# Loads and writes of ternary weight pieces on ScalarE, all seven quarters of the context kept, and another order in the last batch

## The chip, the cores and the metric

The kernel runs on one core of a Trainium2 chip. The metric is the device time of one execution in microseconds (us). The kernel before took 3075.5 us (median of three runs, 3074.82 to 3080.68). The profiled execution took 3074.66 us; its span in the trace is 3072.2 us, so that 2.46 us lie around the span.

The engines are called PE (TensorE, matmuls), PEld (its weight loads), DVE (VectorE), ACT (ScalarE), POOL (GpSimd) and SP (SyncE, which mostly issues DMAs). Each works through its own instructions in a fixed order; a waiting instruction holds up all that stands behind it on its engine.

## The reference

The reference is a model of two layers on `x` (8 batches, 64 rows, 512 columns) and a context `ctx` (8, 1601, 512), with a residual sum around each part:

```python
    x = x + _L0_xattn_ref(_layernorm(x, axis=-1), ctx_1024, mask, Wq, Wkv, Wout, b_out)
    x = x + _L0_attn_ref(_layernorm(x, axis=-1), ...)     # low frequencies attend, high ones are convolved
    x = x + _L0_ffn_ref(_layernorm(x, axis=-1), ...)      # eight experts, a few tokens each
    x = x + _L1_xattn_ref(_layernorm(x, axis=-1), ctx_1024, ctx_1024, ...)
    x = x + _L1_attn_ref(_layernorm(x, axis=-1), ...)     # relative positions
    x = x + _L1_ffn_ref(_layernorm(x, axis=-1), w1, b1, w2, b2)
```

The argument lists are shortened here. Three parts matter for the change. The first cross-attention (16 heads of 64) and the second (16 heads of 32, with a layer norm over each head's queries and keys) both read all of the context. The last part quantizes its two weights (2048 x 512 and 512 x 2048) to three values:

```python
def weight_quant(w):
    scale = 1.0 / jnp.clip(jnp.mean(jnp.abs(w)), 1e-05)
    q = jnp.clip(jnp.round(w * scale), -1.0, 1.0) / scale
    return w + jax.lax.stop_gradient(q - w)
```

So the mean of the absolute values of a whole weight is needed (measure) before any of its elements can be rounded (round).

## The kernel before

The kernel is one program of six stages: `l0_xattn` (0 to about 1505 us in the profile), `l0_attn` (to 1590), the experts (to 1850), `l1_xattn` (to 2907) and a tail with the second layer's attention and feed-forward part (to 3072). A list scheduler decides the order of each engine's instructions from priorities and dependencies; the program text gives the order in which operations become known to it. `tc.keep_in_program_order(ins)` holds one instruction behind the one written just before it on the same engine; the instructions that use its result are not held.

**Quarters.** The large products with the context are done with seven multiplications for two by two blocks in place of eight. For a pair of 128-row blocks of the context the tile `q` holds seven quarters of 128 x 256: four are loaded, and `Quarters.left` (L134 to L139) makes the three others and overwrites one, with four additions on GpSimd. `Quarters.LEFT` (L131) says which of the seven stands where. The matmuls of L468 (scores) and L585 (values) use the quarters, ACT copies some products out of PSUM (`p`, `u` of L428, L531), and DVE adds them up (`s` of L433, `a` of L553 to L568).

**First cross-attention.** The loop at L648 has 17 steps. Step `2*b + half` makes the scores of one half of the heads of batch `b` (`scores`, L420 to L480, six pairs of blocks, run.add once a pair), then its softmax (`softmax` from L496), while the values of the step before are attended (`attend`, L570 to L625, four parts with pieces). `load_columns(b, keep)` (L177) loads the six pairs of the transposed context for a step, 12 DMAs of 256 KB, and has GpSimd make the other quarters, in both halves. In the first half (`keep`) it also writes four of the quarters of each pair to memory (`kept`, two DMAs of 128 and 384 KB a pair). `load_rows` (L194) loads the pairs of the context's rows for the values. Both take their tiles from the same pool of six. The queries, multiplied by the key weight, come through memory as `qk` (L227, 1024 KB), and GpSimd makes their four sums `qt` (L219 to L222).

**The maximum.** `top_of` transposes the running maximum `m` (L449) on PE (`m_ps`, L486), reduces it (`top`, L488) and spreads it with a matmul (`top_ps`, L491); the subtraction (L501) and Exp (L502) follow, and sums that prepare the values (L508 to L511, L515).

**Ternary weights.** The two weights of the last part come in 16 pieces of 512 KB (`TernaryWeights`, L1859). `pass_by` loads a piece from SP into one of two buffers. `measure` (L1887) sums absolute values on ACT (Abs, L1889). `round` (L1900) scales and rounds a piece on DVE (L1904, float32), turns it into bf16 on ACT into the tile `wq` (L1905), limits it to -1 and 1 on DVE (L1906, bf16) and writes it back from SP. There is one buffer of `wq`. `aside(step)` (L363) calls `measure` twice a step in steps 2 to 9 and `round` three times a step in steps 10 to 15; it stands at the end of a step (L668). In the trace these come in bursts: Abs at 240 to 246, 388 to 396 and 415 to 449 us, the rounding at 1015 to 1057, 1074 to 1088 and 1100 to 1147 us.

**Second cross-attention.** `load(b, g)` (L1430) fetches two pairs of blocks (one of three groups of a batch) with eight DMAs: the raw quarters from the input, the made ones from `kept`. The loop over the batches ends (L1802 to L1836) with the work on four score tiles `s[0]` to `s[3]` (four heads each): `scores` (L1684, matmuls of L1691, DVE L1701), `softmax` (a maximum by `fold`, L1709 to L1714, its transpose L1722, `top` L1724, the subtraction L1733, Exp L1734, and a second fold for the total) and `attend` (L1742, with the sum of L1751 and its reciprocal L1754). Three tiles `s` exist. In the last batch (`more` is false) nothing of a next batch stands between these.

Of the kernel before, what the change touches and what calls it, by code (L numbers as in the profile page):

```python
# [123 lines left out]
class Quarters:  # L124
# [5 lines left out]

    LEFT = {1: 0, 2: 1, 3: 6, 4: 3, 5: 4, 6: 5, 7: 2}  # L131

    @staticmethod
    def left(nc, q):  # L134

        nc.gpsimd.tensor_add(q[:, 4, :], q[:, 2, :], q[:, 3, :])  # L136
        nc.gpsimd.tensor_sub(q[:, 5, :], q[:, 4, :], q[:, 0, :])
        nc.gpsimd.tensor_sub(q[:, 2, :], q[:, 0, :], q[:, 2, :])
        nc.gpsimd.tensor_sub(q[:, 6, :], q[:, 1, :], q[:, 5, :])  # L139


def l0_xattn(K, x, d, ternary, kept):
# [7 lines left out]
    with ExitStack() as es:  # L150
# [25 lines left out]

        def load_columns(b, keep=False):  # L177

            pairs = []
            for i in range(NPAIR):  # L180
                q = cp.tile([P, 7, QH], F32, tag="pair", name="ctxT")
                for j in range(2):
                    nc.sync.dma_start(
                        q[:, ds(2 * j, 2), :].rearrange("p h (c n) -> p (h c) n", n=P),
                        d["ctxT"][b, :, ts(2 * i + j, P)].rearrange("(c p) n -> p c n", p=P),
                    )
                Quarters.left(nc, q)
                if keep:
                    nc.sync.dma_start(kept[b][:, i, 3, :], q[:, 2, :])
                    nc.sync.dma_start(kept[b][:, i, 0:3, :], q[:, 4:7, :])  # L190
                pairs.append(q)
            return pairs

        def load_rows(b):  # L194

            pairs = []
            for i in range(NPAIR):
                q = cp.tile([P, 7, QH], F32, tag="pair", name="ctx")
                for j in range(2):
                    nc.sync.dma_start(  # L200
                        q[:, 0:4, :].rearrange("p (h j) n -> p j h n", j=2)[:, j],
                        d["ctx"][b, ts(2 * i + j, P), :].rearrange("p (h n) -> p h n", n=QH),
                    )
                Quarters.left(nc, q)
                pairs.append(q)
            return pairs
# [103 lines left out]
        load_tails(0)  # L310
        ctxT = load_columns(0, True)
        place = [tp.tile([P, 4, 3, QH], F32, tag="pt", name="stage").rearrange("p a b q -> p (a b q)") for _ in range(2)]
# [49 lines left out]

        def aside(step):  # L363
            if 2 <= step < 10:
                for i in range(2):
                    ternary.measure(piece, 2 * (step - 2) + i)
            if step == 10:
                ternary.scales(ps_m.tile([P, 16], F32, tag="mm", name="w_ps"), ones[:, 0:1])
            if 10 <= step < 16:
                for i in range(3 * (step - 10), min(3 * (step - 9), 16)):  # L370
                    ternary.round(piece, zp, i)

# [78 lines left out]
        def scores(b, qkt, ctxT):  # L451
# [12 lines left out]
            for i in range(NPAIR):  # L464

                def mul(ps, n, start, i=i):
                    for e in range(2):
                        nc.tensor.matmul(  # L468
                            ps,
                            lhsT=ctxT[i][:, Quarters.LEFT[n], ts(e, P)],  # L470
                            rhs=right[n][:, e, :],
                            start=start and e == 0,
                            stop=e == 1,
                            skip_group_check=not start,
                        )

                run.add(mul, Scores(s, m, b, i))
                some(2)
            run.end()
            return s, m  # L480
# [89 lines left out]
        def attend(half, s, soft, ctx, o, first):  # L570
# [8 lines left out]
            for part, right in enumerate(parts):  # L579
                pairs = range(3 * part, 3 * part + 3)  # L580
                for m in range(2):
# [22 lines left out]
                    run.add(mul, Mixed(a, m, part == 0, tail))  # L604
                    some(2 * part)
            run.end()
            a5 = a.rearrange("p c (g h q) -> p c g h q", h=2, q=S)
# [40 lines left out]
        for step in range(2 * B + 1):  # L648
            if step < 2 * B:
                b, half = divmod(step, 2)  # L650
                if step:
                    now, ctxT = queries_of(b, half), load_columns(b, half == 0)
                    if half == 0:
                        nc.sync.dma_start(
                            ctxT_tail[:, :, :TAIL], d["ctxT"][b, :, LAST * P :].rearrange("(c p) n -> p c n", p=P)
                        )
                s, m = scores(b, now, ctxT)
                top = top_of(m)
                if step == 1:
                    between = keys_side_of_rest(columns_of(norm_rest, NT - 1))  # L660
# [5 lines left out]
            if step < 2 * B:  # L666
                before = s, softmax(s, top)
            aside(step)  # L668
            if step == 3:
                some(5 * NG)  # L670
            if step and step % 4 == 0:
                project_out(step // 4 - 1, o)
                if step < 2 * B:
                    o = tp.tile([P, NG, 2, S], F32, tag="o", name="o", bufs=1)


# [725 lines left out]
def l1_xattn(K, x, d, ahead, queries_done, in_last, kept):  # L1402
# [7 lines left out]
    with ExitStack() as es:  # L1410
# [19 lines left out]
        def load(b, g):  # L1430

            q = cp.tile([P, 2, 7, QH], F32, tag="ctxT", name="ctxT")
            for u in range(2):
                i = 2 * g + u
                nc.sync.dma_start(
                    q[:, u, 0:2, :].rearrange("p h (c n) -> p (h c) n", n=P),
                    d["ctxT"][b, :, ts(2 * i, P)].rearrange("(c p) n -> p c n", p=P),
                )
                nc.sync.dma_start(
                    q[:, u, 3, :].rearrange("p (c n) -> p c n", n=P),  # L1440
                    d["ctxT"][b, SET:, ts(2 * i + 1, P)].rearrange("(c p) n -> p c n", p=P),
                )
                nc.sync.dma_start(q[:, u, 2, :], kept[b][:, i, 3, :])
                nc.sync.dma_start(q[:, u, 4:7, :], kept[b][:, i, 0:3, :])
            return q
# [237 lines left out]

        def scores(c, r):  # L1684

            s = sp.tile([P, NK, 4, S], F32, tag="s", name="s")
            for k0 in range(0, NK, 2):
# [27 lines left out]

        def softmax(s):

# [13 lines left out]
            for k0, n in (0, 7), (7, NK - 7):  # L1731
                part = s[:, ds(k0, n)]
                nc.vector.tensor_sub(part, part, top.to_broadcast([P, n, 2 * P]))  # L1733
                nc.scalar.activation(part, part, AF.Exp)  # L1734
            total = tp.tile([P, 2 * P], F32, tag="total", name="total")
            fold(s, ALU.add, total)
            return total

        def attend(c, s, total, acc, rs):
# [34 lines left out]
        for b in range(B):  # L1774
# [41 lines left out]
            values(1, 1)  # L1816
            total[2] = softmax(s[2])
            values(2, 0)
            values(2, 1)
            s[1] = scores(1, r_of[1])  # L1820
            keys(0, (0, 1))
            total[1] = softmax(s[1])
            attend(0, s[0], total[0], acc, rs)
            s[3] = scores(3, r_of[3])
            if more:
                queries_of(b + 1, 1)
                queries_of(b + 1, 3)
            keys(0, (2,))
            finish(0)
            attend(2, s[2], total[2], acc, rs)  # L1830
            total[3] = softmax(s[3])
            keys(1, (0,))
            attend(1, s[1], total[1], acc, rs)
            keys(1, (1, 2))
            finish(1)
            attend(3, s[3], total[3], acc, rs)  # L1836
            if b % 2 == 0:
# [21 lines left out]
class TernaryWeights:  # L1859
# [5 lines left out]
    def __init__(self, K, pool, memory, d):  # L1865
        nc = self.nc = K.nc
        self.down = pool.tile([P, 1], F32, tag="wdown", name="wdown")
# [11 lines left out]
    def pass_by(self, piece, i):  # L1879
        w = piece([D], "wraw").rearrange("p a b -> p (a b)")  # L1880
        self.nc.sync.dma_start(self.shaped(w, i), self.from_[i])
        return w
# [3 lines left out]

    def measure(self, piece, i):  # L1887
        w = self.pass_by(piece, i)
        self.nc.scalar.activation(w, w, AF.Abs, accum_out=self.part[:, i // 8, i % 8 : i % 8 + 1])  # L1889
# [9 lines left out]

    def round(self, piece, pool, i):  # L1900
        nc, n = self.nc, i // 8
        w = self.pass_by(piece, i)
        q = pool.tile([P, 1024], BF16, tag="wq", name="wq")
        nc.vector.tensor_scalar(w, w, self.scale[:, n : n + 1], MAGIC, ALU.mult, ALU.add)  # L1904
        nc.scalar.activation(q, w, AF.Identity, bias=self.down, scale=1.0)  # L1905
        nc.vector.tensor_scalar(q, q, 1.0, -1.0, ALU.min, ALU.max)  # L1906
        nc.sync.dma_start(self.to[i], self.shaped(q, i))

# [354 lines left out]
def program(tc, d):  # L2263
    nc = tc.nc
    with tc.tile_pool(name="const", bufs=1) as cp, tc.tile_pool(name="memory", bufs=1, space=DRAM) as memory:
# [4 lines left out]
        slots, done = (memory.tile([CAP * E_, D], F32, tag=n, name=n) for n in ("slots", "done"))  # L2270
        kept = [memory.tile([P, NPAIR, 4, QH], F32, tag=f"kept{b}", name="kept") for b in range(B)]
        l0_xattn(K, x, d, w, kept)
# [128 lines left out]
```

## Time and profile before

| what | us |
|---|---|
| median of three runs (lowest to highest) | 3075.5 (3074.82 to 3080.68) |
| the profiled execution, and its span | 3074.66, span 3072.2 |
| Abs of one piece on ACT (L1889, 16 of them) | 1.057 |
| rounding of one piece: DVE L1904, ACT L1905, DVE L1906 | 0.752, 1.148, 0.426 |
| a DMA issue on ACT | 0.35 to 0.44 |
| one addition of `Quarters.left` on GpSimd (L136, ctxT) | 0.814 |
| from issue to landing, median: ctxT 256 KB, ctx 256 KB, kept written 384 KB | 4.7, 3.2, 2.8 |
| last batch: `m` of the last score tile ready (DVE L1714), last Exp's attend starts | 2888.7, 2895.1 |

The execution was profiled at a mean granted TensorE clock of 0.989 of full speed. The granted clock is half of full speed in these stretches (us): 70.9 to 77.8, 94.8 to 101.7, 1101.8 to 1108.6, 1129.1 to 1132.5, three short ones between 1535 and 1590, 2886.9 to 2900.6, and four more after 2907.

In the profile, "busy" is the time in which an engine executes; issuing a DMA and waiting do not count. A line such as `PE a L1 <- DVE b L2: 4.0, 1, 4.0` says that PE's instruction of line 1 writing `a` found its engine idle and waiting for what DVE did in line 2: 4.0 us in total, once, 4.0 us the longest. In a timeline the first two columns are start and duration, and the bracket is the idle time before with what ended it. 391.76 MB are moved by DMA in an execution.

### The profile page before, as it was taken

To read this page: it belongs to the slowest core of one execution; us is meant where nothing else is said; L and a number is where in the kernel's file an instruction comes from. 1 tells how busy PE (TensorE), PEld (TensorE's weight loads), DVE (VectorE), ACT (ScalarE), POOL (GpSimd) and SP (SyncE) were. 2 spreads that over 40 slices of the span, in tenths; PEclk is the share of its full clock that TensorE was granted. 3 is DMA by queue.
4 is the path that set the end of the run, shared out by engine and by line. 5 is a ranking of instruction groups with operands and counts; after the bars stand their busy time and mean duration, and the time that the engine had idled before them with its cause. 6 is when DMAs were issued, how large, how long until landed. Compare 5 with 4: busy or idle time off the path is not lost.

```text
span 3072.2 us, 41098 instructions
## 1 busy us (share of the span) xinstructions
PE 2979.5 (97%) x15516; PEld 2287.8 (74%) x15521; DVE 1827.7 (59%) x3124; ACT 843.2 (27%) x1618; POOL 993.9 (32%) x959
## 2 busy tenths in 40 slices
PE   8999999999999989999999999999999999999887
PEld 7777768888888768888654446788788888888654
DVE  4845545666656656665443333487676676576648
ACT  2322241222222322222111222233333333323224
POOL 4433343544454534544110002322422404214010
PEclk9999999999999999999999999999999999999899
DMA  8265474434334564432659974212112021030270
GB/s 264 71 198 150 150 245 126 138 104 142 127 103 129 183 192 134 129 116 73 221 186 337 344 265 145 78 30 75 40 54 77 5 89 52 28 89 4 72 122 14
DMA packets 387187, 391.76 MB, mean 128 GB/s; under 512 B 55054, under 2 KB 289558, under 8 KB 385838
## 3 DMA queue, kind: packets, MB, share of 16 engines
q1 hardware_dynamic: 380761, 371.80, 39.4%
q10 hardware_dynamic: 5589, 15.24, 1.4%
q8 instruction: 123, 2.02, 0.3%
q0 software_dynamic: 640, 2.10, 0.2%
q14 instruction: 74, 0.61, 0.1%
HBM read 332.90 MB, written 56.16 MB: 127 GB/s over the span
## 4 chain that ended last, share of the span: by engine, by line
PE 57%; DVE 3%; DMA 2%; ACT 1%; issue 0%; POOL 0%; SPq 0%; POOLq 0%; ACTq 0%; DVEq 0%
PE x_ps L1528 11%; PE y_ps L1528 8%; PE s_ps L1691 6%; PE h_ps L1204 4%; PE oe_ps L1231 4%; PE acc L1742 4%; PE x_ps L585 3%; PE x_ps L468 2%; PE z_ps L585 2%; PE z_ps L468 1%; PE sum_ps L1575 1%; PE y_ps L585 1%; PE y_ps L468 1%; DMA wo<-in_L1x_Wp 1%; PE vt_ps L1619 1%; PE top_ps L1727 1%
## 5 line engine op out<-in xcount | busy, mean ns | idle before, releaser
L1588 POOL TENSOR_TENSOR r<-r,minus_half 128x52 f32<-128x52 f32 x32 | 276.9, 8672 | 559.2 <-DVE r L1587 559.2
L468 PE MATMUL x_ps<-qt,ctxT 128*128 128x256 f32 x1152 | 286.2, 382 | 10.5 <-ACT u L428 7.6
L585 PE MATMUL x_ps<-pt,ctx 128*128 128x256 f32 x1152 | 281.7, 382 | 6.2 <-DVE a L561 4.9
L468 PEld LDWEIGHTS x_ps<-qt,ctxT 128*128 128x128 f32 x1152 | 217.3, 190 | 51.2 <-ACT u L428 10.3
L585 PEld LDWEIGHTS x_ps<-pt,ctx 128*128 128x128 f32 x1152 | 217.2, 190 | 40.2 <-DVE a L561 5.0
L136 POOL TENSOR_TENSOR ctxT<-ctxT 128x256 f32<-128x256 f32 x96 | 78.1, 814 | 415.5 <-DMA ctxT<-in_ctxT 336.0
L1691 PE MATMUL s_ps<-qb,kT 128*128 128x256 f32 x832 | 201.2, 381 | 0.0
L449 DVE TENSOR_TENSOR m<-m,s 128x512 f32<-128x512 f32 x176 | 138.1, 785 | 93.7 <-ACT s L447 91.1
L136 POOL TENSOR_TENSOR ctx<-ctx 128x256 f32<-128x256 f32 x96 | 73.6, 767 | 342.7 <-DMA ctx<-in_ctx 262.6
L1691 PEld LDWEIGHTS s_ps<-qb,kT 128*128 128x128 f32 x832 | 154.2, 190 | 26.2 <-issue 3.5
L501 DVE TENSOR_TENSOR s<-s,top_ps 128x1024 f32<-128x1024 f32 (+1 forms) x112 | 123.2, 1135 | 22.9 <-PE top_ps L491 22.9
L1733 DVE TENSOR_TENSOR s<-s,top_ps 128x1792 f32<-128x1792 f32 x64 | 117.9, 1884 | 28.8 <-PE top_ps L1727 28.8
L433 DVE SCALAR_TENSOR_TENSOR s<-y_ps,bias,p 128x256 f32<-128x256 f32 x96 | 46.3, 483 | 145.9 <-PE y_ps L468 145.1
L1701 DVE TENSOR_TENSOR s<-s_ps,r 128x512 f32<-128x512 f32 x192 | 126.5, 682 | 10.8 <-PE s_ps L1691 10.2
L1734 ACT ACTIVATE s<-s 128x1792 f32<-128x1792 f32 x64 | 101.0, 1591 | 84.0 <-DVE s L1733 84.0
L1742 PEld LDWEIGHTS acc<-s,v 128*64 128x64 f32 x1664 | 97.0, 139 | 32.4 <-issue 27.0
L1742 PE MATMUL acc<-s,v 128*64 128x128 f32 x1664 | 115.8, 282 | 4.1 <-ACT s L1734 4.1
L502 ACT ACTIVATE s<-s 128x1024 f32<-128x1024 f32 (+1 forms) x112 | 110.7, 996 | 29.5 <-DVE s L501 25.4
L1204 PE MATMUL h_ps<-w,tok 128*128 128x512 f32 x256 | 117.3, 593 | 0.0
L1231 PE MATMUL oe_ps<-w,hT 128*128 128x512 f32 x256 | 115.6, 593 | 0.0
L515 DVE TENSOR_TENSOR total<-total,s 128x512 f32<-128x512 f32 x160 | 110.0, 687 | 3.5
L468 PE MATMUL x_ps<-qk,ctxT 128*128 128x256 f32 x384 | 104.4, 389 | 4.1 <-ACT s L447 2.3
(472 smaller groups left out, 6285.4 us busy)
## 6 DMA issues: line engine op xcount, KB each, us to landing
w<-in_L0f_W SPq DMA_DIRECT2D x64, 1024.0 KB, 6.2
ctxT<-in_ctxT SPq DMA_DIRECT2D x240, 256.0 KB, 4.7
ctx<-in_ctx SPq DMA_DIRECT2D x192, 256.0 KB, 3.2
kept<-ctxT SPq DMA_DIRECT2D x48, 384.0 KB, 2.8
ctxT<-kept SPq DMA_DIRECT2D x48, 384.0 KB
wvT<-in_L0x_WvT SPq DMA_DIRECT2D x16, 1024.0 KB, 7.9
qk<-qk_all SPq DMA_DIRECT2D x15, 1024.0 KB, 6.6
qk_all<-stage SPq DMA_DIRECT2D x32, 384.0 KB, 3.5
```

Source lines behind the costliest of these rows:

```text
L136: nc.gpsimd.tensor_add(q[:, 4, :], q[:, 2, :], q[:, 3, :])
L449: nc.vector.tensor_max(self.m, self.m if k else self.s[:, LAST, :], self.s[:, k, :])
L468: nc.tensor.matmul(ps, lhsT=ctxT[i][:, Quarters.LEFT[n], ts(e, P)], rhs=right[n][:, e, :], start=start and e == 0, stop=e == 1, skip_group ...
L501: nc.vector.tensor_sub(s[:, k : k + n], s[:, k : k + n], top.unsqueeze(1).to_broadcast([P, n, HALF]))
L585: nc.tensor.matmul(ps, lhsT=ctx[pair][:, Quarters.LEFT[n], ts(m, P)], rhs=right[n][:, i, :], start=start and i == 0, stop=i == 2, skip_gro ...
L1204: nc.tensor.matmul(ps, lhsT=self.tok[:, c, :], rhs=self.w1[n][:, c, :], start=c == 0, stop=c == DC - 1)
L1231: nc.tensor.matmul(ps, lhsT=self.hT[:, f, :], rhs=self.w2[f // 4][:, f % 4, :], start=f == 0, stop=f == 15)
L1528: nc.tensor.matmul(ps, lhsT=left(n, e), rhs=right(n, e), start=start and e == 0, stop=e == 1, skip_group_check=not start,)
L1588: nc.gpsimd.tensor_tensor(r, r, minus_half, ALU.pow)
L1691: nc.tensor.matmul(ps[:, i].rearrange("p h q -> p (h q)"), lhsT=kT[c][:, ts(k0 + i, P)], rhs=qb[c].rearrange("p h q -> p (h q)"), start=Tr ...
L1701: nc.vector.tensor_mul(out, ps, by)
L1742: nc.tensor.matmul(acc[ds(64 * j, 64), c, :], lhsT=v[:, k, ds(c * P + 64 * j, 64)], rhs=s[:, k, ts(j, P)], start=k == 0, stop=k == NK - 1,)
```

## The change

Three things are changed.

- *Quarters and what is kept.* The seven quarters get another order, made ones in 0 to 2 and loaded ones in 3 to 6, with the same four additions. All seven are written to `kept` in the first half of a batch (one DMA of 896 KB a pair, held behind all 12 loads), the second half loads them from there (one DMA of 896 KB a pair, no addition on GpSimd), and so does the second cross-attention (one DMA of 1792 KB a group). `load_rows` splits its two DMAs by columns and no longer by row blocks.
- *Ternary pieces.* Loads and writes are issued on ACT, the loads held to their place. A generator, started after step 3 and advanced once after each `run.add` in `scores` (six a step) and `attend` (four a step), takes two pieces at a time: two loads, three empty turns (four for rounding), then the two pieces. In `round` the limits come before the rounding, both on DVE in float32, and ACT writes the bf16 values in place into the piece's own buffer; `wq` is gone.
- *The last batch.* Its score tiles are made in another order, the fourth one in a tile of the context pool, and `softmax` is split into `exponentials` and `total_of`.

```diff
-    LEFT = {1: 0, 2: 1, 3: 6, 4: 3, 5: 4, 6: 5, 7: 2}
+    LEFT = {1: 5, 2: 6, 3: 2, 4: 4, 5: 0, 6: 1, 7: 3}
...
-        def load_columns(b, keep=False):
+        def load_columns(b, half=0):
             pairs = []
             for i in range(NPAIR):
                 q = cp.tile([P, 7, QH], F32, tag="pair", name="ctxT")
-                for j in range(2):
-                    nc.sync.dma_start(
-                        q[:, ds(2 * j, 2), :].rearrange("p h (c n) -> p (h c) n", n=P),
-                        d["ctxT"][b, :, ts(2 * i + j, P)].rearrange("(c p) n -> p c n", p=P),
-                    )
-                Quarters.left(nc, q)
-                if keep:
-                    nc.sync.dma_start(kept[b][:, i, 3, :], q[:, 2, :])
-                    nc.sync.dma_start(kept[b][:, i, 0:3, :], q[:, 4:7, :])
+                if half:
+                    nc.sync.dma_start(q, kept[b][:, i])
+                else:
+                    for j in range(2):
+                        nc.sync.dma_start(
+                            q[:, ds(5 - 2 * j, 2), :].rearrange("p h (c n) -> p (h c) n", n=P),
+                            d["ctxT"][b, :, ts(2 * i + j, P)].rearrange("(c p) n -> p c n", p=P),
+                        )
+                    Quarters.left(nc, q)
                 pairs.append(q)
+            if not half:
+                for i, q in enumerate(pairs):
+                    tc.keep_in_program_order(nc.sync.dma_start(kept[b][:, i], q))
             return pairs
...
+        def of_weights():
+            for i in range(0, ternary.PIECES, 2):
+                pieces = [ternary.pass_by(piece, i + j) for j in range(2)]
+                yield from (None,) * 3
+                for j in range(2):
+                    ternary.measure(pieces[j], i + j)
+                    yield
+            ternary.scales(ps_m.tile([P, 16], F32, tag="mm", name="w_ps"), ones[:, 0:1])
+            for i in range(0, ternary.PIECES, 2):
+                pieces = [ternary.pass_by(piece, i + j) for j in range(2)]
+                yield from (None,) * 4
+                for j in range(2):
+                    ternary.round(pieces[j], i + j)
+                    yield
...
                 run.add(mul, Scores(s, m, b, i))
                 some(2)
+                next(aside, None)
...
-            aside(step)
             if step == 3:
                 some(5 * NG)
+                aside = of_weights()
...
             q = cp.tile([P, 2, 7, QH], F32, tag="ctxT", name="ctxT")
-            for u in range(2):
...
+            nc.sync.dma_start(q, kept[b][:, ts(g, 2)])
             return q
...
-        def scores(c, r):
-            s = sp.tile([P, NK, 4, S], F32, tag="s", name="s")
+        def scores(c, r, spare=False):
+            if spare:
+                s = cp.tile([P, 2, 7, QH], F32, tag="ctxT", name="s").rearrange("p u k (h q) -> p (u k) h q", q=S)
+                s = s[:, :NK]
+            else:
+                s = sp.tile([P, NK, 4, S], F32, tag="s", name="s")
...
+            else:
+                s[1] = scores(1, r_of[1])
+                total[2] = softmax(s[2])
+                values(2, 0)
+                s[3] = scores(3, r_of[3], True)
+                values(2, 1)
+                exponentials(s[1])
+                attend(0, s[0], total[0], acc, rs)
+                exponentials(s[3])
+                total[1] = total_of(s[1])
+                attend(2, s[2], total[2], acc, rs)
+                total[3] = total_of(s[3])
+                for c in (1, 3):
+                    attend(c, s[c], total[c], acc, rs)
...
     def pass_by(self, piece, i):
         w = piece([D], "wraw").rearrange("p a b -> p (a b)")
-        self.nc.sync.dma_start(self.shaped(w, i), self.from_[i])
+        self.tc.keep_in_program_order(self.nc.scalar.dma_start(self.shaped(w, i), self.from_[i]))
         return w
...
-    def round(self, piece, pool, i):
+    def round(self, w, i):
         nc, n = self.nc, i // 8
-        w = self.pass_by(piece, i)
-        q = pool.tile([P, 1024], BF16, tag="wq", name="wq")
-        nc.vector.tensor_scalar(w, w, self.scale[:, n : n + 1], MAGIC, ALU.mult, ALU.add)
+        q = w.bitcast(BF16)[:, :1024]
+        nc.vector.tensor_scalar(w, w, self.scale[:, n : n + 1], 1.0, ALU.mult, ALU.min)
+        nc.vector.tensor_scalar(w, w, -1.0, MAGIC, ALU.max, ALU.add)
         nc.scalar.activation(q, w, AF.Identity, bias=self.down, scale=1.0)
-        nc.vector.tensor_scalar(q, q, 1.0, -1.0, ALU.min, ALU.max)
-        nc.sync.dma_start(self.to[i], self.shaped(q, i))
+        nc.scalar.dma_start(self.to[i], self.shaped(q, i))
```

## The prediction

> **What bounds the kernel now.** I read the shares of the engines, then the chain that ended last, the windows by stage, and the waits of TensorE (PE) and ScalarE (ACT) with their timeline.
>
> ```profile
> PE 2979.5 (97%) x15516; PEld 2287.8 (74%) x15521; DVE 1827.7 (59%) x3124; ACT 843.2 (27%) x1618; POOL 993.9 (32%) x959
> PE 57%; DVE 3%; DMA 2%; ACT 1%; issue 0%; POOL 0%; SPq 0%; POOLq 0%; ACTq 0%; DVEq 0%
> ```
>
> PE is busy for 2979.5 of 3072.2 us and leads the chain; no matmul is added or removed. Time can therefore be won only where PE stands idle (92.7 us in all) or runs at a lowered clock. Work taken off GpSimd, SyncE (SP) or VectorE (DVE) counts only where PE waits for it. Windows (us; busy time of PE, PEld, DVE, ACT, POOL; granted clock; DMA share; GB/s):
>
> ```profile
> 66.00:102.00 36.00, 26.63 (x94) 19.72 (x93) 27.96 (x35) 10.25 (x17) 21.83 (x24) 0.81 0.26 74
> 400.00:500.00 100.00, 94.81 (x458) 73.56 (x457) 52.95 (x85) 32.19 (x64) 36.89 (x48) 1.00 0.68 219
> 600.00:700.00 100.00, 99.80 (x513) 85.11 (x512) 60.51 (x95) 23.96 (x51) 50.70 (x64) 1.00 0.35 103
> 1000.00:1100.00 100.00, 94.56 (x487) 78.36 (x485) 66.45 (x113) 29.55 (x50) 49.67 (x62) 1.00 0.59 183
> 1100.00:1200.00 100.00, 91.89 (x455) 75.54 (x456) 60.28 (x104) 28.12 (x49) 35.04 (x42) 0.95 0.49 154
> 2846.00:2903.00 57.00, 46.93 (x352) 38.64 (x351) 45.30 (x64) 12.80 (x15) 0.17 (x2) 0.88 0.02 3
> ```
>
> A steady stretch (600:700) leaves PE 0.20 us idle in 100. The poor stretches are the start, the two where ternary pieces are handled, and the last batch. The waits of PE, then one of ACT, then PE's timeline:
>
> ```profile
> PE x_ps L468 <- ACT u L428: 7.6, 6, 4.2
> PE x_ps L585 <- DVE a L561: 4.9, 1, 4.9
> PE m_ps L1722 <- DVE m L1714: 4.8, 1, 4.8
> PE acc L1742 <- ACT s L1734: 4.1, 2, 3.0
> PE y_ps L468 <- DVE s L433: 4.0, 1, 4.0
> PE x_ps L468 <- DMA qk<-qk_all: 1.8, 1, 1.8
> ```
> ```profile
> ACT wq L1905 <- DMA w_out<-wq: 34.2, 10, 16.1
> ```
> ```profile
> 1102.39 2.93 PE L585 MATMUL x_ps<-pt,ctx 128*128 128x256 f32 x6 [4.85 <-DVE a L561]
> 1128.20 1.26 PE L468 MATMUL x_ps<-qt,ctxT 128*128 128x256 f32 x4 [4.21 <-ACT u L428]
> ```
>
> ACT waits for the single wq buffer to be written out; the copies that PE needs stand behind it in ACT's order. That is how 4.85 and 4.21 us reach PE.
>
> **The change, part by part** (the sum starts from the profiled run's 3074.66 us: span 3072.2 and 2.46 around it; the median is 0.84 higher).
>
> *1. Ternary pieces.* What they cost now: in 1000:1200 PE idles 5.44 + 8.11 = 13.55 us, and the clock of 0.95 in the second hundred costs some 100 x 0.05 = 5; less 0.4 of steady idle that is 18.2. In 400:500, 5.19 us idle, of which about 2.2 lie at the matmuls of L254 and L461 that no piece delays: 3.0. In 200:300 PE is busy 98.57, so 1.3 beyond steady. Together 22.5 us.
>
> What they will cost: ACT issues two loads, then soon runs what needs them. `keep_in_program_order` holds the loads, not their users. In the changed instruction order the Abs (or Identity) mostly stands one or two copies behind its loads, sometimes next to them; about 3 us of PE work lie between. A 512 KB load lands 4.3 us after issue:
>
> ```profile
> wraw<-in_L1f_w1T SPq DMA_DIRECT2D x16, 512.0 KB, 4.3
> w_out<-wq SPq DMA_DIRECT2D x16, 256.0 KB, 4.1
> ```
>
> Queued behind the waiting Abs are ACT's copies out of PSUM (u, p of L428), for which PE waits; behind the waiting DVE rounding stand the sums of L433 and L561. Upper bound: each of 16 pairs (8 measured, 8 rounded) stalls PE by 4.3 - 3.0 = 1.3, 21 us. Lower bound: as the cheap bursts of today, where 13 Abs in 415:449 cost PE 3.0 us (0.23 each) and ten roundings in 1015:1060 about 3.0 (0.3 each): 16 x 0.23 + 16 x 0.3 = 8.5. Between them I take 0.8 a pair, 13 us: the u copy has some 1.7 us of slack before PE misses it, so that a part of each 1.3 is covered, not all. The wait for wq's write disappears, since bf16 now lies in the piece and two pieces rotate. Gain 22.5 - 13 = 9.5, between 1.5 and 14. The extra DVE time (two operations of 0.752, L1904, for 0.752 + 0.426, L1906: 16 x 0.33 = 5 us) lies in DVE's 41% of free time, its cover in a steady stretch being 39.5 us per 100.
>
> *2. Start.* Step 1's pairs now come finished from memory. GpSimd is silent from 66 to 78, where it now makes three pairs while DVE's maxima (L449) take 1.17 to 1.24 instead of 0.68; and the top matmul no longer stands behind a score matmul that waits 1.8 us for qk. Directly: about 1.0 (two maxima) + 1.8 = 2.8. The DVE queue of the softmax (busy without a break from 77.43 to 99.6) then ends earlier by the same and by what GpSimd slowed L508 to L510 (1.30 to 1.48 against 0.94: 1.4), so the 4.0 us wait for L433 shrinks, and half clock from 94.8 to 101.7 (3.4 us lost) may go. Gain 5, between 0 (qk, now competing with 896 KB loads, lands later by all of it) and 8.
>
> *3. Last batch.* In 2846:2903 DVE works 45.30 us of 57, idle 11.7, while PE waits for DVE or ACT: a maximum, its transpose, a subtraction, Exp and a sum of the third score tile follow one another with nothing beside them. Scored early, this chain runs beside the attend matmuls of the other tiles. By hand, DVE's work of 45.3 remains and the waits before `top` and before the subtraction (2.9 + 3.2) and for scores (2.7) go, other small ones staying: idle about 3.2 to 4. Gain 11.7 - 4.2 = 7.5, between 4 (only m's 4.8 less one shorter wait) and 10. The spare tile is one of the context groups, free by then.
>
> *4. Memory and queues.* A first half issues 6 writes of 896 KB in place of 12 of 128 and 384 KB, behind all 12 loads; a second half 6 loads of 896 KB for 12 of 256 KB, and 24 GpSimd operations fewer (192 in all, about 0.8 us each). About 37 MB more move beside 391.76 MB. On SP the writes wait for GpSimd, and the context rows queue behind them; but pairs are asked for as buffers come free, a step ahead: step 1's last pair is issued at 69.76, and its turn comes five pairs of 6 us after 80.9, 41 us later. In step 0 the loads of pairs 3 to 5 (issued from 30.7, after writes that waited for GpSimd) come some 10 us earlier, but PE has no gap there to win. An L1 group is issued at 1950 to 2000 and needed in the next batch. 48 issues on ACT at 0.35 to 0.44 us are 19 us, spread over eight steps in which ACT is 24 to 32% busy. I cost all this at 0; a pair that came 2 us late in each of 16 steps would cost 32.
>
> Sum: 3074.66 - 9.5 - 5 - 7.5 = 3052.7, so **3053**.
>
> Two rules of the Trainium skill. Row: after the 4.85 us gap the granted clock is half from 1101.8 to 1108.6. "TensorE: Matmul & The Clock Gate", Part 1, says an idle window of about 3.4 us halves the clock; by it, stalls of at most 1.3 us would never halve it and item 1's 5 us of clock would all be won, as the sum has it. Row: w1T loads in 400:460 land in 6.4 us, against 4.3 over the run. "DMA: Bandwidth & Descriptors", "Issuing engines are not separate DMA queues", says loads of any engine share the same 16 DMA engines and only issue time is saved; by it, moving pieces to ACT wins no landing time, which speaks against item 1 and for the last rival.
>
> **Rivals.**
> B: *uses that run forward give the ternary gain back.* Each pair pays 1.3 (21 us): 3074.66 - 1.5 - 5 - 7.5 = 3061; with start and last batch at their low ends, 3069. For: no pin on the users. Against: today's cheap bursts.
> C: *pieces hidden wholly:* 3074.66 - 22.5 - 5 - 7.5 = 3040. For: in a few places (attend) 7.8 us of work lie between. Against: most have 3.
> D, the slower side: *late landings on ACT.* If 512 KB loads meet bursts of 896 KB, every pair's stall grows by the landing beyond 4.3. 16 x d = 21.7 eats the gain at d = 1.36 (landing 5.7); from d = 1.74 (landing 6.0) it is slower by over 0.2%; at 7 us it is 3053 + 16 x 2.7 = 3096. For: 6.4 in 400:460, a burst. Against: 4.3 over all 16, and now pieces come two at a time.
>
> **How the numbers follow.** A, the forecast, 0.58, own range 3043 to 3063; B 0.18; C 0.10; D 0.14. 0.2% is 6.15 us, about what this kernel's runs can tell. Slower: 0.12 (D beyond 6.0 us). Same: 0.08 of B and 0.02 of D. Faster: 0.78. The range from 3039 (C's end) to 3071 (B's end) leaves out D and little else.
>
> **What would show it.** Right: 1000:1200 at clock 1.00 with PE busy above 193; waits of ACT on `wraw` of about 1 us a pair; no top matmul behind qk; 2846 to the last Exp shorter by 7. Wrong: ACT waits on `wraw` above 2 us a pair, PE waiting for ctxT, ctx or kept at all, or a new gap in the last batch behind Exp of the spare tile.

## The result, and the profile after

The changed kernel takes 3093.87 us (median of 19 runs, 3081.41 to 3110.55) against 3077.15 us for the kernel before on the same chips (19 runs, 3072.72 to 3083.15). The ratio is 1.0054, with a 95% interval of 1.0041 to 1.0066: slower by half a per cent, where 3053 us and "faster" were forecast. The profiled execution took 3084.65 us (span 3082.9), 10 us more than that of before; it is one of the quicker ones, so that the profile shows the smaller part of the loss.

The page's busy times and the shares of the chain, as shown of before:

```profile
PE 2980.6 (97%) x15516; PEld 2294.4 (74%) x15521; DVE 1820.9 (59%) x3124; ACT 843.8 (27%) x1618; POOL 845.8 (27%) x767
PE 88%; DMA 5%; DVE 4%; ACT 1%; issue 1%; POOL 0%; SPq 0%; POOLq 0%; ACTq 0%; DVEq 0%
```

PE does the same work; GpSimd (POOL) does 148 us less. DMA has risen from 2% to 5% of the chain. Where the time went is seen best by marking the same matmul in both traces: the first score matmul of the context's tail in a step (L461 before, L472 after), and later marks. The table is read off PE's timelines; the lag is after less before.

| mark | before, us | after, us | lag, us |
|---|---|---|---|
| step 1 | 77.18 | 73.70 | -3.5 |
| step 3 | 284.00 | 277.12 | -6.9 |
| step 5 | 496.83 | 491.50 | -5.3 |
| step 8 | 749.87 | 763.97 | +14.1 |
| step 11 | 1014.22 | 1043.99 | +29.8 |
| step 13 | 1208.69 | 1230.05 | +21.4 |
| last batch, first scores | 2686.07 | 2706.66 | +20.6 |
| first matmul of the tail | 2900.76 | 2912.81 | +12.1 |
| last matmul | 3068.07 | 3078.71 | +10.6 |

The start gives 6.9 us and the last batch 8.5, both near the forecast. (The last batch's mark is not quite the same place in both: before, the tail's first matmul stands ahead of the batch's last sums, at 2902.89; after, it stands behind them, at 2912.70. At the first matmul of the output projection, L1776 after, the lag is +8.9.) Between steps 3 and 13, where the pieces are handled, 28.2 us are lost instead of 9.5 won. Windows of the kernel after, the last one the last batch, with the columns as before:

```profile
400.00:500.00 100.00, 96.11 (x463) 77.99 (x462) 52.42 (x84) 24.20 (x49) 22.64 (x28) 0.97 0.56 206
500.00:600.00 100.00, 91.69 (x466) 77.45 (x464) 53.03 (x85) 25.60 (x52) 40.63 (x52) 0.97 0.47 162
600.00:700.00 100.00, 95.27 (x480) 80.48 (x481) 55.98 (x91) 27.56 (x57) 26.02 (x33) 0.97 0.44 152
700.00:800.00 100.00, 91.97 (x469) 77.69 (x468) 56.47 (x93) 25.30 (x50) 43.28 (x56) 0.98 0.49 171
1100.00:1200.00 100.00, 95.75 (x481) 80.66 (x480) 64.95 (x109) 30.18 (x54) 43.95 (x54) 0.97 0.50 168
2858.00:2915.00 57.00, 50.30 (x385) 43.46 (x384) 52.36 (x79) 14.34 (x19) 0.25 (x2) 0.96 0.07 21
```

The stretch 600:700, steady before (99.80 busy at clock 1.00), is now among the poor ones: the stalls that stood in two bursts are spread over eight steps, and each stretch pays in idle time and in clock. In the last batch PE's busy time rose from 46.93 to 50.30 of 57 us, the clock from 0.88 to 0.96. The waits of PE:

```profile
PE x_ps L479 <- ACT s L458: 22.1, 7, 8.6
PE m_ps L498 <- DVE m L460: 15.0, 12, 3.5
...
PE acc L1756 <- ACT s L1742: 3.4, 1, 3.4
...
PE s_ps L472 <- DMA qk<-qk_all: 0.9, 1, 0.9
```

The first two name an ACT copy and a DVE maximum which were themselves late. Behind what they stood, the waits of ACT and then of DVE say:

```profile
ACT wraw L1933 <- DVE wraw L1932: 39.3, 13, 8.4
ACT wraw L1917 <- DMA wraw<-in_L1f_w2T: 18.0, 7, 6.4
ACT wraw L1917 <- DMA wraw<-in_L1f_w1T: 13.6, 7, 3.7
```
```profile
DVE wraw L1931 <- DMA wraw<-in_L1f_w1T: 13.1, 4, 5.2
DVE wraw L1931 <- DMA wraw<-in_L1f_w2T: 9.6, 4, 4.5
```

In 22 of the 32 pieces the first user waits for the load. The worst place shows how this reaches PE. ACT's timeline, then PE's, then SP's:

```profile
587.60 1.73 ACTq L1910 DMA_DIRECT2D wraw<-in_L1f_w2T  x2
...
590.97 0.37 ACT L439 COPY p<-z_ps 128x256 f32<-128x256 f32 x1 [1.15 <-PE z_ps L479]
597.74 1.06 ACT L1917 ACTIVATE wraw<-wraw 128x1024 f32<-128x1024 f32 x1 [6.40 <-DMA wraw<-in_L1f_w2T]
598.70 0.19 ACT L1917 ACTIVATION_READ_ACCUMULATOR wraw<-wraw 128x1 f32 x1
601.40 1.06 ACT L1917 ACTIVATE wraw<-wraw 128x1024 f32<-128x1024 f32 x1 [2.52 <-DMA wraw<-in_L1f_w2T]
602.37 0.19 ACT L1917 ACTIVATION_READ_ACCUMULATOR wraw<-wraw 128x1 f32 x1
602.46 0.46 ACT L458 ACTIVATE s<-x_ps,bias 128x256 f32<-128x256 f32 x1
```
```profile
602.97 2.07 PE L479 MATMUL x_ps<-qk,ctxT 128*128 128x256 f32 x4 [8.58 <-ACT s L458]
```
```profile
580.66 10.86 SPq L194 DMA_DIRECT2D kept<-ctxT  x6
592.69 17.70 SPq L203 DMA_DIRECT2D ctx<-in_ctx  x4
```

Two copies after their issue at 587.60 ACT stands before the pieces; they are there 10.1 and 13.4 us after issue, not 4.3, because SP's six writes of 896 KB and the context rows run at the same time. The score copy (L458) that PE needs is behind both. The view of DMA for 585:610 shows the engines full until about 601: 40 slices of 0.625 us, the first row in tenths busy, the second over 400 GB/s in most of the first twenty.

```profile
DMA  9999999999999999999998999610001000000000
GB/s 433 424 424 424 436 424 424 413 447 413 418 418 403 423 428 431 403 398 449 419 428 315 390 393 387 225 49 7 0 0 26 0 0 0 0 0 0 0 0 0
```

### The profile page after: what moved, and what is told of

Same layout as the page of the kernel before. It is cut to its first block, busy times and chain, and to the rows that moved or that the text cites. A ratio compares the mean times of both kernels' runs of the same rounds, so it can differ in the third digit from the quotient of the medians.

```text
span 3082.9 us, 40423 instructions
## 1 busy us (share of the span) xinstructions
PE 2980.6 (97%) x15516; PEld 2294.4 (74%) x15521; DVE 1820.9 (59%) x3124; ACT 843.8 (27%) x1618; POOL 845.8 (27%) x767
## 4 chain that ended last, share of the span: by engine, by line
PE 88%; DMA 5%; DVE 4%; ACT 1%; issue 1%; POOL 0%; SPq 0%; POOLq 0%; ACTq 0%; DVEq 0%
PE x_ps L1532 11%; PE x_ps L597 11%; PE x_ps L479 10%; PE y_ps L1532 8%; PE s_ps L1699 6%; PE z_ps L597 5%; PE z_ps L479 5%; PE oe_ps L1246 4%; PE h_ps L1219 4%; PE acc L1756 3%; PE y_ps L597 3%; PE y_ps L479 2%; PE s_ps L472 2%; DMA wraw<-in_L1f_w2T 2%; DMA wraw<-in_L1f_w1T 1%; PE v_ps L631 1%
## 5 line engine op out<-in xcount | busy, mean ns | idle before, releaser
L460 DVE TENSOR_TENSOR m<-m,s 128x512 f32<-128x512 f32 x176 | 131.4, 746 | 118.6 <-ACT s L458 115.9
L1709 DVE TENSOR_TENSOR s<-s_ps,r 128x512 f32<-128x512 f32 x192 | 126.8, 682 | 12.6 <-PE s_ps L1699 10.3
L479 PEld LDWEIGHTS x_ps<-qk,ctxT 128*128 128x128 f32 x384 | 71.7, 194 | 47.0 <-ACT s L458 24.9
```

The source lines that it names most:

```text
L460: nc.vector.tensor_max(self.m, self.m if k else self.s[:, LAST, :], self.s[:, k, :])
L479: nc.tensor.matmul(ps, lhsT=ctxT[i][:, Quarters.LEFT[n], ts(e, P)], rhs=right[n][:, e, :], start=start and e == 0, stop=e == 1, skip_group ...
L1709: nc.vector.tensor_mul(out, ps, by)
```

## The experiments

All are compared with the kernel before on the same chip. Two theories stood at the outset: that users of pieces wait for late loads (1), and that the larger traffic or ACT's queue costs PE time in itself (2).

**e1: the users held to their places too.** In `measure` and `round`:

```diff
-        self.nc.scalar.activation(w, w, AF.Abs, accum_out=...)
+        self.tc.keep_in_program_order(self.nc.scalar.activation(w, w, AF.Abs, accum_out=...))
...
+        self.tc.keep_in_program_order(nc.vector.tensor_scalar(w, w, self.scale[:, n : n + 1], 1.0, ALU.mult, ALU.min))
...
+        self.tc.keep_in_program_order(nc.scalar.activation(q, w, AF.Identity, bias=self.down, scale=1.0))
```

> The changed kernel with the first user of every piece (Abs on ACT, the first DVE operation, Identity on ACT) held to its place in the program as the loads are, so that 12 to 15 ACT instructions stand between loads and use. Theory 1 (the slowdown is ACT and DVE waiting in front of pieces that have not landed; PE lost some 51 us to it in the profile, 39 idle and 12 by the clock): the waits on wraw fall to near nothing and the time falls below both kernels, 3077 - 7 (start) - 12 (last batch) - 22 (stalls of before) + 5 to 10 = about 3041 to 3047. Theory 2 (the larger kept traffic or the ACT queue itself costs PE the time): stays above 3080.

Measured: 3039.11 us (3035.70 to 3040.61), ratio 0.9872 (0.9858 to 0.9887). This is faster than both kernels, as theory 1 had it. Loads and users now stand 18 to 58 us apart in the timelines. Windows of e1:

```profile
400.00:500.00 100.00, 99.44 (x489) 80.63 (x488) 55.43 (x88) 26.11 (x53) 24.09 (x28) 1.00 0.61 218
600.00:700.00 100.00, 99.38 (x512) 84.36 (x510) 58.23 (x94) 28.49 (x59) 31.60 (x41) 1.00 0.46 158
1000.00:1100.00 100.00, 99.24 (x545) 82.68 (x544) 63.80 (x100) 24.91 (x50) 42.09 (x52) 1.00 0.54 182
```

Beside 182 GB/s and a DMA share of 0.54 PE is now 0.76 us idle in 100: traffic costs next to nothing where no one stands in front of it. The only wait on a piece that is left is ACT's for DVE's second operation:

```profile
ACT wraw L1935 <- DVE wraw L1934: 31.8, 12, 6.9
```

and PE loses next to nothing by it: from 380 to 1230 us the waits of PE for another engine come to 5.2 us in e1, 40.6 in the kernel after. Between steps 3 and 13 e1 wins 23.3 us on the kernel before (lag -5.8, then -29.2) where the kernel after loses 28.2: some 51 us, which is what the pieces cost in the changed kernel's profile. By the medians e1 is 54.8 us faster than the kernel after.

**e2: the pieces as before, the rest as changed** (`aside`, SP loads, `wq` and SP writes restored).

> The changed kernel with the ternary pieces handled as before (bursts, SP loads and writes, wq), everything else as changed. Theory 1: keeps the gains of the start (7) and of the last batch (12), 3077 - 19 = about 3058. Theory 2 (the kept traffic costs): 3075 or more.

Measured: 3047.42 us (3046.44 to 3055.31), ratio 0.9904 (0.9890 to 0.9919). Theory 2 falls again; the gain is 11 us more than expected. Its lag falls from -6.7 at step 9 to -13.7 at step 13: the old bursts of rounding cost 7 us less beside the new loads. ACT's wait for the write of `wq` is shorter too (28.0 us in all and 8.3 the longest, against 34.2 and 16.1); that the new loads issue fewer DMAs on SP, the queue that carries the write, may be why, but was not tested.

**e3: four of seven quarters kept**, written by one DMA of 512 KB a pair and not held; second halves load from the input and use GpSimd.

```diff
-                if half:
-                    nc.sync.dma_start(q, kept[b][:, i])
...
+                Quarters.left(nc, q)
+                if not half:
+                    nc.sync.dma_start(kept[b][:, i], q[:, 0:4, :])
```

> The changed kernel with four of seven quarters kept (written by one 512 KB DMA a pair, not held), the second half loading 256 KB pieces and using GpSimd again; pieces on ACT and last batch as changed. Theory 1a (pieces land late because the 896 KB transfers fill the DMA engines): pieces' waits fall to about 1 us a pair, their cost to 15 to 20 us: 3077 - 12 - 5 = 3060 to 3068. Theory 1b (the users stand too near the loads, with whatever traffic): still 40 us or more, 3083 or more.

Measured: 3076.66 us (3070.23 to 3082.38), ratio 0.9994 (0.9983 to 1.0005): between the two. The start's gain is gone (lag -0.8 at step 3), and from there to step 13 it loses 4.8 us. Measured from e1, whose pieces cost nothing and which wins 23.3 us on the same way, the pieces cost 28 us here and 51 in the kernel after. But e1 keeps seven quarters; the fairer measure is e7 below, which holds the users with four quarters kept: by the medians the pieces cost 22.7 us with four (e3 less e7) and 54.8 with seven. So both theories hold a part: more than half of the cost comes with the traffic of all seven quarters, the rest is there without it. The pair in the place of the worst one above is used 4.6 and 5.5 us after issue, not 10.1 and 13.4.

**e4: the old order in the last batch.**

> The changed kernel with the order of the last batch as before. If the last batch gained what the traces show (lag 23.45 us before it, 12.05 us after it), this run is 11 to 12 us above the changed kernel: about 3096 when that is at 3085, 3110 when at 3099. If the gain came from elsewhere: no difference.

Measured: 3092.22 us (3090.07 to 3098.21), ratio 1.0043 (1.0031 to 1.0056), which can't be told from the kernel after: the scatter of the pieces' stalls (29 us between the runs of the kernel after) covers 11 us. Its trace shows the old wait of 4.83 us for `m` again. e8 repeats it where it can be told.

**e5: each write to `kept` behind its own pair, not held behind all loads.**

> The changed kernel, only that each 896 KB write to kept stands behind its own pair (three writes after each six loads) and is not held behind all 12 loads; same bytes. Theory burst (late landings come from the row of six writes): the two pairs that waited longest (use 10 to 13 and 9 to 12 us after issue) fall to 7 or less, PE wins about 10 us: about 3084. Theory bytes (it is the traffic as such, the context rows' loads as much as the writes): no clear change from the changed kernel's 3094, within 5 us.

Measured: 3091.28 us (3082.62 to 3113.19), ratio 1.0049 (1.0032 to 1.0067). Both theories missed a term. The two worst pairs did fall (first users at 4.5 and 5.3 us after issue, second at 9.7 and 9.5), and between steps 3 and 13 it loses 18.2 instead of 28.2 us. But the start pays it back: its lag at step 3 is +4.2 instead of -6.9, since three writes that wait for GpSimd again stand ahead of the last six loads. SP is through with them 6.2 us later (its first store of `qk_all` goes out at 46.60 us instead of 40.37), and at step 1 PE waits 5.49 us for `qk` instead of 0.94. Holding the writes back is worth 11 us there.

**e6: the pieces' loads on SP**, users free; one word differs from the kernel after.

```diff
-        self.tc.keep_in_program_order(self.nc.scalar.dma_start(self.shaped(w, i), self.from_[i]))
+        self.tc.keep_in_program_order(self.nc.sync.dma_start(self.shaped(w, i), self.from_[i]))
```

> The changed kernel with the pieces' loads issued on SP (held there to their place), users still free, writes still on ACT. Theory queue (two loads on ACT's queue run beside SP's transfers and share the DMA engines with them; on SP's own queue they run in turn and land in about 4 us, as they did before): stalls of at most about 1.3 us a pair, 3077 - 6 - 11 - 22 + 21 = about 3059. Theory place (users too near, whichever queue): 3085 or more.

Measured: 3047.86 us (3043.40 to 3051.37), ratio 0.9903 (0.9889 to 0.9916), better than either expected. Where the first user of a pair waited for its piece, it came 4.2 to 5.4 us after issue in six of nine cases, and 10.2 to 11.2 in three, but those stood so late that they waited at most 1.0 us. In the trace those three were issued on SP right behind its writes to `kept` or its loads from there. Waits of DVE and ACT in e6:

```profile
DVE wraw L1931 <- DMA wraw<-in_L1f_w2T: 9.0, 6, 3.1
ACT wraw L1917 <- DMA wraw<-in_L1f_w1T: 5.8, 4, 4.5
DVE wraw L1931 <- DMA wraw<-in_L1f_w1T: 5.6, 2, 3.2
ACT wraw L1917 <- DMA wraw<-in_L1f_w2T: 3.6, 3, 1.5
```

They come to 24.0 us, against 54.3 in the kernel after, and PE's cost from step 3 to 13 is 10 us (lag -18.9 where e1 has -29.2). So this run doesn't show that SP's queue as such lands sooner: with the queue the scheduler's order changed too, the loads go out ahead of the context rows and their users stand in other places. Queue and place changed together, and which of them won how much stays open.

**e7 and e8: four quarters, and the old last batch, each with the users held.**

> The held users of e1 with four of seven quarters kept as in e3. With the pieces hidden, the keeping of all seven should show what it is worth by itself: start 6 (lag at step 3: -6.9 with it, -0.8 without) and the second cross-attention's loads 2 to 3: 3039 + 8 to 9 = about 3047. Rival: the larger traffic costs what it saves, 3039.

Measured for e7: 3053.94 us (3044.95 to 3059.48), ratio 0.9918 (0.9903 to 0.9934): keeping all seven is worth 14.8 us beside e1, more than the 8 to 9 expected. Its profile runs behind e1's by 4.2 us at step 3, 9.1 at step 13 and 10.8 when the experts begin, each mark with what came before it. That profiled run is 5.5 us above its median, so the marks show where the loss arises better than how large it is.

> The held users of e1 with the last batch's order as before: the price of that order where nothing else varies. By the marks of the traces (last batch to the first tail matmul: 214.7 us before, 212.8 with the old order and the new loads, 206.2 to 206.6 with the new order) 6.3 to 6.7 us more than e1: about 3046. Rival: the tail swallows it, 3039 to 3041.

Measured for e8: 3043.60 us (3039.61 to 3048.75), ratio 0.9895 (0.9880 to 0.9910): the new order is worth 4.5 us by the medians, though the intervals of e1 and e8 just overlap. At the tail's first matmul it is ahead by 6.5 (lags -39.7 and -33.2), at the last matmul by 4.3 (-38.7 and -34.4). At the output projection between them it is ahead by 10.3: in the old order some of the tail's work already stands ahead of the batch's last sums, so that part of the gain is work moved and not saved.

**e9: the pieces' part of the change alone, on the kernel before.**

> The kernel before with the ternary pieces' part of the change alone (loads and writes on ACT, generator, in-place bf16), four quarters kept and the old last batch. Theory: the pieces' part alone loses, about what e3's profile shows (27 us for the pieces, against 22 before): 3077 + 5 = about 3082. Rival (the pieces are harmed only by the larger kept traffic): stalls at most 1.3 us a pair, and the burst's clock loss gone: 3060 to 3070.

Measured: 3081.65 us (3073.66 to 3087.02), ratio 1.0020 (1.0010 to 1.0029): this part alone loses, as theory 1 had it.

**e10: pieces one at a time on ACT.**

> The changed kernel with pieces loaded one at a time on ACT (one load, two empty turns, its use) in place of two. Theory pair (two loads issued together share the engines, the second lands 1 to 3 us later): a third of the stalls goes, 3094 - 15 = about 3079. Rival (what counts is SP's traffic beside them, and 32 waits replace 16): 3089 or more.

Measured: 3085.91 us (3083.61 to 3092.01), ratio 1.0036 (1.0022 to 1.0050), between the two. The medians differ by 8 us from the kernel after and the loss between steps 3 and 13 is 19.3 us instead of 28.2, but the intervals overlap, and the users stand in other places too. That two loads share the engines is a part at most.

**e11: users held and loads on SP; e12: users held, pieces' part alone on the kernel before.**

> The held users of e1 with the pieces' loads on SP. Theory: with 12 or more instructions between load and use the queue no longer matters: 3039 within 4. Rival: the loads on SP hold up the context rows or stand late themselves: 3046 or more.

> The kernel before with the pieces' part of the change and the users held as in e1, nothing else of the change (four kept, old last batch). Theory: pieces cost nothing then, so the 22 us of stalls that the pieces cost before go: 3077 - 22 = about 3055. Rival (without the quieter SP of the new loads the pieces still land late, or the 48 DMA issues on ACT cost something themselves): 3062 or more.

Measured: e11 3038.18 us (3034.97 to 3040.56), ratio 0.9873 (0.9858 to 0.9888), the same as e1. e12 3054.21 us (3050.43 to 3057.98), ratio 0.9918 (0.9903 to 0.9932). With distance between load and use the queue doesn't matter, the 32 load issues on ACT cost nothing that can be told (the 16 writes are on ACT in both), and the stalls that the pieces cost in the kernel before come out as 24.4 us (its lag at step 13; 1.4 of it is there at step 2, before the first piece is loaded).

The parts don't add up singly:

| what is in the kernel | users free | users held |
|---|---|---|
| pieces on ACT alone (e9, e12) | 3081.7 | 3054.2 |
| with the new last batch (e3, e7) | 3076.7 | 3053.9 |
| and all seven quarters kept (the change, e1) | 3093.9 | 3039.1 |

Keeping all seven quarters wins 15 us when the users are held and loses 17 when they are not. (The middle row also has the new order of the quarters and one write a pair, and e7's runs scatter over 14 us, so that it is no measure of the last batch; e8 is. The runs come from several chips, on which the kernel before took 3077.0 to 3080.1 us.)

## Why the prediction was wrong

*Item 1, the pieces: wrong, and it decided.* The prediction's term was 0.8 us a pair, 13 us, under an upper bound of 1.3 a pair ("4.3 - 3.0"). Measured: 51 us, 3.2 a pair, above the bound. The prediction's own sign of being wrong, ACT waiting on `wraw` for more than 2 us a pair, came: 31.6 us over the eight measured pairs. The count of 16 pairs, the 3 us of work between load and use, and the row of waiting (Abs before copies before PE) were right. The failed step is the landing: 4.3 us was the median of loads issued on SP, behind SP's other transfers, most of them one at a time, and the trace of before gives a landing for only 4 of the 32 (4.0 to 6.4), so that "4.3 over all 16" rests on three loads. It was carried over to pairs of loads on ACT that start at once, beside whatever SP has under way. There the first user came 3.8 to 10.1 us after issue and the second 5.1 to 13.4 where they waited; that second wait was no part of the bound. With the larger traffic away the cost falls from 54.8 to 22.7 us (e3 and e7); e10, with one load at a time, is 8 us faster, which the intervals don't tell apart; e6, with the loads back on SP (and so in other places), won 46. Still, 22.7 us is more than the 13 forecast: the users are too near without that traffic as well. The 22.5 us that the pieces cost before were right (e12: 24.4).

*The clock.* The sum had item 1's 5 us of clock all won, since stalls of at most 1.3 us "would never halve it". The stalls were longer, and less than 3.4 us was enough: a gap of 2.41 us was followed by 3.4 us at half clock. The measurement decides here against the rule that the prediction cites, and the trace of before showed it already: from 67.5 to 70.9 us PE was busy for 1.13 of 3.40 us, with no gap over 1.86, and the clock was half from 70.9. From 380 to 1230 us half clock makes up 37.5 us (10.2 before).

*Item 2, the start: right in mechanism, and near in size.* Gain 6.9 us against 5. The top matmul (at 71.60 us) no longer stands behind the score matmul that waits for `qk`, and of two stretches of 6.8 us at half clock one of 3.4 is left. e3, without the kept quarters, has 0.8 of the gain. e5 shows that it hangs on the held writes as well: with them spread, `qk` comes late, which is the low end that the prediction named, and the gain turns into a loss of 4.2.

*Item 3, the last batch: mechanism right, size open.* PE's wait of 4.8 us for `m` is gone. The stretch to the tail's first matmul shrank by 8.5 us (7.5 forecast), but 1.9 of that is there with the old order too (e4). From the last batch's first scores to the last matmul the new order wins 7.75 us in the kernel after (beside e4) and 3.25 in e1 (beside e8); by e8's median it is 4.5.

*Item 4, memory and queues at 0: wrong in both directions.* With users held it wins 15 us, item 2's start included; with users free it costs 17, through the pieces and not through a context pair (PE waits for no `ctxT` or `ctx` in the profile after). The prediction had its price only in rival D and gave D 0.14.

*The rivals.* D happened: late landings on ACT, priced at 3096 for a landing of 7 us; 3093.87 was measured. That the numbers lie so close is partly luck: 7 us was an example, and the price had no loss of clock in it. C, pieces wholly hidden (3040), is e1 (3039.11), again with other parts: the kept quarters give 15 us there, where C had 5 for the start. What spoke for D was weighed too lightly: the one burst in the trace with 6.4 us, and the Trainium skill's "DMA: Bandwidth & Descriptors", "Issuing engines are not separate DMA queues", whose rule that DMAs started by any engine interleave on the same 16 DMA engines agrees with the trace here: with SP's transfers filling the engines from 585 to 601 us, the two loads on ACT were used 10.1 and 13.4 us after issue. What spoke against it, 4.3 over all pieces, came from the queue that was being left.

## What to carry to other kernels

A landing time belongs to the traffic beside and ahead of the load; when a load moves to another engine's queue, price it beside the largest transfer that can be under way, not by its old median, and see how many landings that median rests on. Holding the loads to their places gained nothing here while their users were free: look in the final instruction order at what stands between them, above all on an engine that others wait for. And a change of several parts is to be priced with the parts together: the kept quarters gained 15 or lost 17 us according to how three instructions were placed.

## What the runs showed of the hardware

The clock fell without a window in which PE was idle throughout. Clock changes lie 3.41 us, or multiples of it, apart; cut into such windows, the kernel after has these (the clock is that of the window itself):

```profile
535.20:538.60 3.40, 0.99 (x7) 0.81 (x7) 0.83 (x2) 1.81 (x4) 0.00 (x0) 1.00 1.02 368
538.60:542.00 3.40, 3.40 (x14) 3.02 (x13) 1.43 (x3) 0.85 (x2) 2.27 (x2) 0.50 0.14 49
890.20:893.60 3.40, 0.68 (x3) 0.63 (x4) 3.33 (x5) 1.77 (x3) 3.40 (x4) 1.00 0.35 121
893.60:897.00 3.40, 3.40 (x10) 2.71 (x9) 2.71 (x4) 1.41 (x2) 3.32 (x4) 0.50 0.34 131
```

PE was busy for 0.99 and 0.68 of 3.40 us, and the next window ran at half clock, though PE was then fully busy. Over the 14 profiles (before, after and twelve experiments), leaving out the first 10 us, all 111 such windows at full clock with PE busy for less than 42% were followed by half clock, 22 of 58 between 42% and 53%, and 16 of 201 between 53% and 75%. Above 75% it was 26 of some 11,860, several of them with PE busy throughout, so the share of busy time in the trace doesn't decide it alone; what counts as busy for the clock is not shown here. So a stall of some 2 us costs up to 1.7 us more when it falls within one window.

Why the 19 runs of the changed kernel scatter over 29 us where the four of e1 scatter over 5 isn't settled. That it goes with free users is not shown: e7, with users held, scatters over 14.5 us in six runs, and e6, with users free, over 8 in five.
